# Recommender kernel: recorded instructions with semaphores of the kernel's own, and six more columns of token rows fetched by SyncE and ScalarE

## The chip, the cores and the metric

One core of a Trainium2 chip runs the program. A core has five engines that run side by side: TensorE (PE), VectorE (DVE), ScalarE (ACT), GpSimd (POOL) and SyncE (SP), each with an instruction stream of its own, and 16 DMA engines that move data between the memory of the chip and the core. Engines wait for each other by semaphores. The metric is the device time of one execution in microseconds; lower is better.

## The reference

16,384 examples, each with 32 token indices, three lists of 20 indices and four single indices. What is computed:

```python
tok = word_emb[token_idx].mean(axis=1)          # 32 rows of 300 floats out of 50000, per example
e1, e2, e3 = emb_mh1[mh1_idx].mean(axis=1), ...  # 20 rows of 64 out of 1000, 5000, 10000
o1, o2, o3, o4 = emb_oh1[oh1_idx], ...           # one row of 64 each
emb = concatenate([tok, e1, e2, e3, o1, o2, o3, o4], axis=1)        # 748 wide
wide = sums of the one-column tables wide_mh*, wide_oh* at the same indices
h = relu(emb @ W1 + b1); h = relu(h @ W2 + b2); h = relu(h @ W3 + b3)   # 1024, 512, 256
return sigmoid(h @ Wd + bd + wide)
```

All in float32. The token rows are the bulk of what is moved: 16,384 x 32 rows of 1200 bytes.

## The kernel before, in words

The examples are cut into 128 tiles of 128, one example per partition. A tile takes 11 steps of a main loop of 1435 steps in all (27 of them are the end). In a step several things are emitted for different tiles, so that the engines overlap:

- **Small tables** are not gathered. Per step DVE builds one-hot rows (`one_hots`, tile `hot`), ACT scales a part of them in place (by 256), PE multiplies them into counts (`counts`, tile `pc`), and ACT evicts these to `cnt`. A tile later PE multiplies the counts with the tables on chip (`small_sums`, tile `pg`), and DVE reduces the result into the features `g`.
- **Token rows** come by `tokens()`. A column is one of the 32 token positions of a tile: 128 indices, one row of 300 floats for each partition. POOL issues one indirect DMA (a gather) per column into half of a `tok_rows` buffer; there are six buffers of two columns, and DVE adds the two halves of a pair into `tok_sum` (in tile `own`, `add_up`) three pairs later in program order. 1.42 pairs per step are emitted.
- **Fetched columns** spare POOL a gather. For some tiles SP (`fetch`, column 31) or ACT (`ScalarRows`, column 30) loads the 128 indices as offsets into registers (a TENSOR_LOAD of 32 or 8 values) and issues 128 DMAs of one row each, into `fetched` or `fetched_scalar`. Ahead of it the column of indices is loaded and DVE turns it into byte offsets (`column_offsets`). SP is paced at 128 rows in 16.5 steps. ACT's rows are put in wherever the next transfer would take one of two places of a count modulo 8 (`sync_dma`, `hardware_dma`).
- **Layers** (`mlp`) run for one to three tiles at once on PE in float32, with ACT evicting.

The order of every engine but POOL is that of the emitting code. The semaphores are the framework's: hardware transfers take eight of them in turn (LANES; SP's rows come to use 0 to 5, ACT's 6 and 7), the gathers eight others, and a transfer waits for the one before it in its lane.

## Time and profile before

| | |
|---|---|
| median of three runs | 7429.4 us (7415.1 to 7435.34) |
| span of the profiled execution, first to last instruction | 5019.3 us |
| time of that execution beside its span | not given; median less span is 2410.1 us |
| gathers on POOL | 3987, 946 ns each |
| row DMAs of SP, of ACT | 10624, 3328 |
| granted TensorE clock, mean | 0.990 |

The span covers the program's own instructions. Busy time counts the engines' work, not the issuing of a transfer by a sequencer and not waiting; rows with SPq or ACTq are such issues. "Idle before" is the time in which an engine did nothing ahead of an instruction, put down to the event that stood last before its start.

### The profile page before, as it was taken

To read this page: it belongs to the slowest core of one execution; us is meant where nothing else is said; L and a number is where in the kernel's file an instruction comes from. 1 tells how busy PE (TensorE), PEld (TensorE's weight loads), DVE (VectorE), ACT (ScalarE), POOL (GpSimd) and SP (SyncE) were. 2 spreads that over 40 slices of the span, in tenths; PEclk is the share of its full clock that TensorE was granted. 3 is DMA by queue.
4 is the path that set the end of the run, shared out by engine and by line. 5 is a ranking of instruction groups with operands and counts; after the bars stand their busy time and mean duration, and the time that the engine had idled before them with its cause. 6 is when DMAs were issued, how large, how long until landed. Compare 5 with 4: busy or idle time off the path is not lost.

```text
span 5019.3 us, 124363 instructions
## 1 busy us (share of the span) xinstructions
PE 4806.3 (96%) x36356; PEld 3721.3 (74%) x36356; DVE 3748.7 (75%) x6830; ACT 2726.5 (54%) x3658; POOL 3774.2 (75%) x3994
## 2 busy tenths in 40 slices
PE   6799999999999999999999999999999999999999
PEld 4577777777777777777777777667767888888899
DVE  6777777777777777777777777777777777777774
ACT  5455555555555555555555555555555555555552
POOL 7777777777777777777777777777777777777775
PEclk8899999999999999999999999999999999999999
DMA  7444444444444444444444444444444444444443
GB/s 204 127 129 130 129 129 129 129 130 129 129 130 128 129 130 129 130 129 129 129 129 129 130 129 129 130 129 129 130 130 129 129 129 130 130 129 130 129 128 100
DMA packets 291735, 654.13 MB, mean 130 GB/s; under 512 B 147100, under 2 KB 161692, under 8 KB 291048
## 3 DMA queue, kind: packets, MB, share of 16 engines
q0 software_dynamic: 191376, 612.66, 45.1%
q1 hardware_dynamic: 89271, 29.49, 2.7%
q10 hardware_dynamic: 10400, 4.02, 0.4%
q8 instruction: 284, 4.65, 0.4%
q14 instruction: 404, 3.30, 0.2%
HBM read 645.65 MB, written 0.07 MB: 129 GB/s over the span
## 4 chain that ended last, share of the span: by engine, by line
PE 37%; DMA 26%; DVE 15%; issue 12%; POOL 9%; ACT 1%; SPq 1%; ACTq 0%; DVEq 0%; POOLq 0%
DMA tok_rows<-in_word_emb_dram,it 23%; PE ph L677 17%; PE pg L554 14%; POOL tok_rows L337 9%; DVE hot L501 5%; DVE own L319 4%; PE pc L519 4%; DVE own L314 3%; DMA fetched_scalar<-in_word_emb_dram 1%; DMA fetched<-in_word_emb_dram 1%; PE pc L595 1%; DVE g L544 1%; PE po L719 1%; SPq L161 1%; DVE x L599 0%
## 5 line engine op out<-in xcount | busy, mean ns | idle before, releaser
L337 POOL DMA_INDIRECT tok_rows<-in_word_emb_dram,it x3987 | 3773.3, 946 | 1219.3 <-issue 754.1
L508 ACT ACTIVATE hot<-hot 64x768 bf16<-64x768 bf16 (+1 forms) x1408 | 1155.4, 821 | 1820.6 <-DVE hot L501 1664.0
L554 PE MATMUL pg<-terms,cnt 128*128 128x195 bf16 x17664 | 1723.7, 249 | 35.6 <-DVE g L544 35.0
L554 PEld LDWEIGHTS <-cnt 128*128 128x128 fp8e3 x17664 | 1529.2, 98 | 83.1 <-issue 54.4
L677 PE MATMUL ph<-x,w_sb 128*128 128x384 f32 (+5 forms) x4932 | 1473.8, 437 | 16.2 <-ACT h L688 11.9
L501 DVE TENSOR_TENSOR hot<-own,sc 128x1656 bf16<-128x1656 bf16 (+1 forms) x1408 | 1393.7, 990 | 126.7 <-PE pc L519 37.7
L522 ACT ACTIVATE cnt<-pc 128x828 uint16<-128x828 f32 (+1 forms) x1408 | 1186.5, 843 | 181.5 <-PE pc L519 103.2
L319 DVE TENSOR_TENSOR own<-own,tok_rows 128x300 f32<-128x300 f32 x1792 | 857.1, 478 | 513.3 <-DMA tok_rows<-in_word_emb_dram,it 468.5
L677 PE MATMUL ph<-h,w_sb 128*128 128x384 f32 (+2 forms) x4160 | 1225.9, 435 | 14.2 <-ACT h L688 14.0
L314 DVE TENSOR_TENSOR own<-own,tok_rows 128x300 f32<-128x300 f32 x1827 | 873.8, 478 | 271.9 <-DMA tok_rows<-in_word_emb_dram,it 221.0
L677 PEld LDWEIGHTS ph<-x,w_sb 128*128 128x128 f32 (+1 forms) x4932 | 830.8, 191 | 305.7 <-ACT h L688 23.0
L519 PEld LDWEIGHTS <-hot 128*128 128x128 bf16 x8192 | 594.2, 98 | 523.8 <-issue 271.3
L677 PEld LDWEIGHTS ph<-h,w_sb 128*128 128x128 f32 x4160 | 700.6, 191 | 266.1 <-ACT h L688 27.3
L519 PE MATMUL pc<-hot 128*128 128x138 bf16 x8192 | 733.1, 225 | 111.8 <-ACT hot L508 51.7
L688 ACT ACTIVATE h<-ph,b_sb 128x384 f32<-128x384 f32 (+2 forms) x723 | 378.7, 524 | 210.5 <-PE ph L677 115.4
L544 DVE TENSOR_REDUCE g<-pg 128x130 f32<-128x390 f32 (+1 forms) x512 | 259.2, 506 | 140.0 <-PE pg L554 138.7
L599 DVE TENSOR_TENSOR x<-pc,scale 128x768 f32<-128x768 f32 x127 | 120.8, 951 | 58.8 <-PE pc L595 57.5
L595 PE MATMUL pc<-ident,g 128*128 128x128 f32 x762 | 107.3, 278 | 5.7 <-ACT cnt L522 5.4
L312 DVE TENSOR_TENSOR own<-tok_rows 128x300 f32<-128x300 f32 x128 | 61.5, 481 | 55.3 <-DMA tok_rows<-in_word_emb_dram,it 52.6
L595 PEld LDWEIGHTS pc<-ident,g 128*128 128x128 f32 x762 | 83.7, 143 | 9.8 <-ACT cnt L522 9.3
L488 DVE COPY sc<-pc 128x512 bf16<-128x512 bf16 x64 | 44.0, 688 | 40.5 <-PE pc L484 39.8
L719 PE MATMUL po<-h,wd_sb 128*1 128x384 f32 (+2 forms) x208 | 67.4, 442 | 4.4 <-ACT h L688 4.4
(59 smaller groups left out, 514.6 us busy)
## 6 DMA issues: line engine op xcount, KB each, us to landing
fetched<-in_word_emb_dram SPq DMA_DIRECT2D x10624, 1.2 KB
tok_rows<-in_word_emb_dram,it POOLq DMA_INDIRECT x3987
fetched_scalar<-in_word_emb_dram ACTq DMA_DIRECT2D x3328, 1.2 KB
ix<-in_idx_dram SPq DMA_DIRECT2D x64, 64.0 KB
w_sb<-in_W_dram SPq DMA_DIRECT2D x6, 512.0 KB
raw<-in_mh_dram SPq DMA_DIRECT2D x4, 682.5 KB
it<-in_idx_dram SPq DMA_DIRECT2D x64, 32.0 KB
w_sb<-in_W_dram SPq DMA_DIRECT2D x1, 2048.0 KB
```

Source lines behind the costliest of these rows:

```text
L314: nc.vector.tensor_add(tok_sum, tok_sum, a)
L319: nc.vector.tensor_add(to, tok_sum, b)
L337: gather = nc.gpsimd.indirect_dma_start(out=rows[-1], out_offset=None, in_=word, in_offset=bass.IndirectOffsetOnAxis(ap=it[:, j : j + 1], ...
L501: nc.vector.tensor_tensor(hot[:, 0 : 2 * rows, :].rearrange("p i (n d) -> p i n d", d=2), iota.rearrange("p (n d) -> p n d", d=2).unsqueez ...
L508: nc.scalar.activation(upper, upper, AF.Copy, scale=UPPER)
L519: nc.tensor.matmul(pc[:, k // n, at : at + n_h], hot[:, 2 * k, 0:P], hot[:, 2 * k + 1, :], start=True, stop=True)
L522: nc.scalar.activation(cnt[:, :, b : b + rows].rearrange("l h (g k) -> l h g k", g=2), pc[:, :, 0 : n * n_h].rearrange("l g (k h) -> l h g ...
L544: nc.vector.tensor_reduce(field_columns(features(t), pair), pg[:, 0:n, :].rearrange("p f (c d) -> p f d c", c=3), AX.X, ALU.add,)
L554: nc.tensor.matmul(pg[:, j, :], by_slice[:, h, :], terms[:, h, :], start=(h == h0), stop=(h == h1 - 1))
L595: nc.tensor.transpose(pt[:, j // n, j % n, :], g[:, c : c + P], ident)
L677: nc.tensor.matmul(to, weights[: src.shape[0], k, m * P : (m + 1) * P], src, start=(k == 0), stop=(k == len(srcs) - 1),)
L688: nc.scalar.activation(dst()[:, m, 0:n], ph[:, 0:n], AF.Relu, bias=bias[:, m : m + 1])
```

## The change

All instructions are now recorded first, each with the regions that it reads and writes (`Program.record`), and then emitted in one block (`Program.emit`) with semaphores that the kernel allots itself. Per engine there is one semaphore, raised only by instructions that somebody waits for; a wait that is already implied by an earlier one is left out. The gathers have one semaphore per `tok_rows` buffer, which both gathers of a pair raise; rows of a fetched column have one of eight semaphores per engine, raised by all 128 rows, and no row waits for another. The other hardware transfers still take eight lanes in turn. PE's bf16 and fp8 weight loads are no longer entries of their own but part of their matmul.

SP and ACT are given their columns by a table made ahead (`RowFetches`): column after column without a pause, each for the first free tile that still leaves the margin. SP fetches 84 columns at the same 16.5 steps each; ACT 31, three rows in every step, two ahead of the scaling of `hot` and one behind it. 3981 gathers are left on POOL. The order of PE's matmuls and ACT's activations is that of before, and DVE's too but for the small offset instructions.

```diff
-    def hardware_dma(queue, **operands):
-        dma = queue.dma_start(**operands)
-        if transfers and transfers[-1][0] is not queue:
-            tc.add_manual_dep(...)
-        transfers.append((queue, dma.ins.name))
     def sync_dma(**operands):
-        while len(transfers) % LANES in SCALAR_LANES and scalar_row and scalar_row[0]():
-            pass
-        hardware_dma(nc.sync, **operands)
+        return program.dma(core.sync, **operands)
...
-                tok_rows = tokp.tile([P, TOK_GROUP * TOK_D], F32, name="tok_rows")
+                tok_rows, batch = tokp.next(), []
...
-                    gather = nc.gpsimd.indirect_dma_start(...)
-                    tc.stamp_issue_order_token(gather.ins, "gathers")
+                    program.gather(f"gather{tokp.slot}", rows[-1], word, it[:, j : j + 1], batch, tok_rows)
...
+    def gather(self, lane, out, table, index, batch, buffer):
+        def emit():
+            return self.nc.gpsimd.indirect_dma_start(...)
+        return self.record(emit, "POOL", lane, [index], [out if batch else buffer], batch=batch)
...
+        def need(other):
+            other = other.batch[-1]
+            if other.batch is ins.batch:
+                return
+            if other.stream == ins.stream and stream == "PE":
+                return
+            best = needed.get(other.stream)
+            if best is None or best.tick < other.tick:
+                needed[other.stream] = other
...
+        known = self.known[sequencer]
+        waits = [o for s, o in needed.items() if known.get(s, 0) < o.tick]
...
+    def fetch(t, j, by_scalar, loads):
+        queue, ring = (core.scalar, fa) if by_scalar else (core.sync, fp)
+        tile_rows = ring.next()
+        lane = f"{'ACT' if by_scalar else 'SP'}rows{rings[by_scalar] % ROW_SEMAPHORES}"
+        column, batch = columns.pop((t, j)), []
+        for p0 in range(0, P, loads):
+            values = program.load(queue, column[:, p0 : p0 + loads], last_offset)
+            yield 0
+            for p in range(p0, p0 + loads):
+                program.row(queue, lane, rows[p : p + 1, :], lambda values=values: values.pop(0), word_bytes, batch)
...
-    fetches = [(summed_at(t) - FETCH_AHEAD[t % 3], t) for t in range(FETCH_FROM, tiles) if t % 3]
+    by_sync = RowFetches(N_TOK - 1, False, summed_at(FETCH_FROM) - FETCH_STEPS - FETCH_MARGIN, FETCH_STEPS, tiles, LOADS)
+    by_scalar = RowFetches(
+        N_TOK - 2, True, int(summed_at(SCALAR_FROM) - scalar_steps - SCALAR_MARGIN), scalar_steps, tiles - 2, SCALAR_LOADS
+    )
...
+            by_sync.prepare(step)
+            by_scalar.prepare(step)
+            scalar_rows(step, SCALAR_BEFORE)
             if i < STEPS - 1:
                 hot = one_hots(sc, s, i + 1)
...
+            scalar_rows(step, SCALAR_AFTER)
-            fetch_rows(step, 0.5)
+            sync_rows.to(step + 0.5)
```

The first gathers of the program in POOL's queue, before (DMASW0 to 7 are the gathers' lanes, DMAHW0 that of the index transfer; the ending _49 belongs to the framework's names):

```order
L337 DMA tok_rows<-in_word_emb_dram,it 128x300 [waits DMAHW0_49]
L337 DMA tok_rows<-in_word_emb_dram,it 128x300 x7
L337 DMA tok_rows<-in_word_emb_dram,it 128x300 [waits DMASW0_49]
L337 DMA tok_rows<-in_word_emb_dram,it 128x300 [waits DMASW1_49]
L337 DMA tok_rows<-in_word_emb_dram,it 128x300 [waits DMASW2_49]
L337 DMA tok_rows<-in_word_emb_dram,it 128x300 [waits DMASW3_49]
L337 DMA tok_rows<-in_word_emb_dram,it 128x300 [waits DMASW4_49,DVE_49]
L337 DMA tok_rows<-in_word_emb_dram,it 128x300 [waits DMASW5_49]
L337 DMA tok_rows<-in_word_emb_dram,it 128x300 [waits DMASW6_49,DVE_49]
```

and the same place now (tok_rows_61 to 66 are the six buffers):

```order
L244 DMA tok_rows_61<-in_word_emb_dram,it_67 128x300 [waits sem_lane0]
L244 DMA tok_rows_61<-in_word_emb_dram,it_67 128x300
L244 DMA tok_rows_62<-in_word_emb_dram,it_67 128x300 x2
L244 DMA tok_rows_63<-in_word_emb_dram,it_67 128x300 x2
L244 DMA tok_rows_64<-in_word_emb_dram,it_67 128x300 x2
L244 DMA tok_rows_65<-in_word_emb_dram,it_67 128x300 x2
L244 DMA tok_rows_66<-in_word_emb_dram,it_67 128x300 x2
L244 DMA tok_rows_61<-in_word_emb_dram,it_67 128x300 [waits sem_DVE]
L244 DMA tok_rows_61<-in_word_emb_dram,it_67 128x300
```

Before, seven gathers follow the first without a wait, and from the ninth on each waits for the one eight places back, every second one for DVE too; now the first of a pair waits for DVE, and the second for nothing.

DVE in the middle of the program, before, where the two adds of a pair are the lines 314 and 319:

```order
L501 TENSOR_TENSOR hot<-own,sc 128x1656 [waits DVE_49,PE_49,Activation_49]
L314 TENSOR_TENSOR own<-own,tok_rows 128x300 [waits DMASW5_49,DVE_49]
L319 TENSOR_TENSOR own<-own,tok_rows 128x300 [waits DMASW6_49,DVE_49]
L314 TENSOR_TENSOR own<-own,tok_rows 128x300 [waits DMASW7_49,DVE_49]
L319 TENSOR_TENSOR own<-own,tok_rows 128x300 [waits DMASW0_49,DVE_49]
```

and now (all engines' instructions carry the line of the recorder, L112):

```order
L112 TENSOR_TENSOR hot_77<-own,sc_74 128x1656
L112 TENSOR_TENSOR own<-own,tok_rows_61 128x300 [waits sem_gather0,sem_DVE]
L112 TENSOR_TENSOR own<-own,tok_rows_61 128x300 [waits sem_DVE]
L112 TENSOR_TENSOR hot_76<-own,sc_74 128x1656 [waits sem_PE]
L112 TENSOR_TENSOR own<-own,tok_rows_62 128x300 [waits sem_gather1,sem_DVE]
```

Each add waited for its own gather; now the first add of a pair waits for both gathers, the second for DVE alone.

ACT in the middle of the program, before (DMAHW6 and 7 are the lanes left to it):

```order
L508 ACTIVATE hot<-hot 64x6x128 [waits DVE_49]
L375 TENSOR_LOAD columns
L688 ACTIVATE h_51810<-ph,b_sb 128x384 [waits PE_49]
L522 ACTIVATE cnt<-pc 128x138x6 [waits PE_49]
L161 DMA fetched_scalar<-in_word_emb_dram 1x1200 [waits DMAHW6_49]
L161 DMA fetched_scalar<-in_word_emb_dram 1x1200 [waits DMAHW7_49]
L508 ACTIVATE hot<-hot 64x6x128 [waits DVE_49]
```

and now (`odd` is the buffer of the first layer's result):

```order
L112 ACTIVATE cnt_78<-pc_94 128x138x6 [waits sem_ACT,sem_PE]
L238 DMA fetched_scalar_82<-in_word_emb_dram 1x1200 x2
L112 ACTIVATE hot_76<-hot_76 64x6x128 [waits sem_DVE]
L259 TENSOR_LOAD columns
L238 DMA fetched_scalar_82<-in_word_emb_dram 1x1200
L112 ACTIVATE cnt_78<-pc_94 128x138x6 [waits sem_PE]
```

The rows have lost their waits and stand at fixed places around `hot`; most count evictions have got a wait for an earlier one of ACT's own.

533 lines of the change are left out of this document (353 added, 180 removed).

## Prediction

> **What bounds the kernel now.** I read the page's head first, then the groups of instructions, then the timeline of POOL, and only then the waits of the other engines. The page's head:
>
> ```profile
> span 5019.3 us, 124363 instructions
> PE 4806.3 (96%) x36356; PEld 3721.3 (74%) x36356; DVE 3748.7 (75%) x6830; ACT 2726.5 (54%) x3658; POOL 3774.2 (75%) x3994
> ```
>
> By busy time PE looks like the bound (4806.3 of 5019.3) and POOL like an engine with a quarter to spare. The groups and the view of one tile, `tok_rows`, say otherwise (columns of the first: count, busy us, mean ns, idle before it; of the second: shortest/median/longest ns, first and last start in us):
>
> ```profile
> L337 POOL DMA_INDIRECT tok_rows<-in_word_emb_dram,it x3987 | 3773.3, 946 | 1219.3 <-issue 754.1 <-DVE own L319 222.3 <-DVE own L314 78.3
> ...
> L337 POOL DMA_INDIRECT tok_rows<-in_word_emb_dram,it x3987: 942/946/1233, 2.8 to 4993.1; - x200
> ```
>
> Idle time of 1219.3 us over 3987 gathers is 0.306 us for each, and from the first start to the last there are (4993.1 - 2.8) / 3986 = 1.252 us per gather. So is the idle time a wait? The waits of POOL, and its timeline at the start of the program, answer it:
>
> ```profile
> POOL tok_rows L337 <- issue: 754.1, 2473, 0.3
> POOL tok_rows L337 <- DVE own L319: 222.3, 721, 2.7
> POOL tok_rows L337 <- DVE own L314: 78.3, 257, 0.3
> ...
> 2.84 1.10 POOL L337 DMA_INDIRECT tok_rows<-in_word_emb_dram,it  x1 [1.36 <-DMA it<-in_idx_dram]
> 4.25 0.95 POOL L337 DMA_INDIRECT tok_rows<-in_word_emb_dram,it  x1 [0.30 <-issue]
> 5.50 0.94 POOL L337 DMA_INDIRECT tok_rows<-in_word_emb_dram,it  x1 [0.30 <-issue]
> 6.74 0.94 POOL L337 DMA_INDIRECT tok_rows<-in_word_emb_dram,it  x1 [0.30 <-issue]
> ...
> 12.99 0.95 POOL L337 DMA_INDIRECT tok_rows<-in_word_emb_dram,it  x1 [0.30 <-issue]
> 14.24 0.94 POOL L337 DMA_INDIRECT tok_rows<-in_word_emb_dram,it  x1 [0.30 <-issue]
> ```
>
> Nearly every gap is 0.30 us whichever event stands beside it, and 721 gaps "for DVE" hold 222.3 us, 0.308 each. The first eight gathers, which wait for no buffer and no earlier gather (the order of POOL shows it), stand at the same 1.25 us as the later ones that wait for one or two semaphores. So 1.25 us is what a gather costs POOL, and POOL issues without a pause from 2.8 us to 4993.1 us: 3986 x 1.25 = 4982.5 of the 4990.3 us between. What is over, some 8 us, has one visible piece near the end:
>
> ```profile
> 4929.22 0.95 POOL L337 DMA_INDIRECT tok_rows<-in_word_emb_dram,it  x1 [0.30 <-issue]
> 4932.82 0.94 POOL L337 DMA_INDIRECT tok_rows<-in_word_emb_dram,it  x1 [2.65 <-DVE own L319]
> ```
>
> The span is then 2.8 us of start, 4990.3 us of gathers, and 26.2 us after the last gather's start, in which the last tile goes through the layers. Everything else follows POOL: DVE, which adds the rows up, sits waiting for rows to land, and ACT waits for DVE.
>
> ```profile
> DVE own L319 <- DMA tok_rows<-in_word_emb_dram,it: 468.5, 683, 2.8
> DVE own L314 <- DMA tok_rows<-in_word_emb_dram,it: 221.0, 333, 3.1
> ...
> ACT hot L508 <- DVE hot L501: 1664.0, 1089, 5.0
> ...
> 2000.00:2500.00 500.00, 488.05 (x3557) 358.57 (x3555) 378.71 (x688) 274.05 (x356) 378.02 (x401) 0.99 0.48 129
> ```
>
> The last row (a stretch of 500 us: PE, PEld, DVE, ACT, POOL busy, then PE clock, DMA share, GB/s) has 401 gathers in 500 us, 1.247 each, with PE at 488 of 500. PE is the next bound, 2.4% behind.
>
> **What lies around the span.** The page gives no time of the profiled execution besides its span. The median of the runs shown is 7429.4 us, 2410.1 us above that span, and no row of the trace shows what fills the difference. I carry it over as a constant; what it could do otherwise is a rival below. The page "Runtime: NRT & Kernel Launch" of the Trainium skill, section "The ~15µs preamble/postamble breakdown", puts about 9 to 15 us around a kernel, which as an estimate from that page would make the time some 5034 us; the runs measured 7429.4, so the measurement decides, and the page doesn't explain the rest.
>
> **The change, part by part.** *Fewer gathers.* SP fetches 84 columns instead of 83 (10624 rows in the trace / 128), ACT 31 instead of 26 (3328 / 128), so POOL issues 4096 - 115 = 3981 gathers instead of 3987. Six gathers at 1.25 us are 7.5 us, all of it on the bound. The place of a fetched column doesn't matter, as POOL has no other work to wait for.
>
> *Fewer semaphores on POOL.* Of 2032 wait-only instructions 1973 go, and the second gather of a pair waits for nothing. Bounds: nothing, by the eight gathers at the start that have no waits and the same 1.25 us; and, from the other side, all 0.306 us of every gap. The rows at 4.25 to 6.74 us are the very thing that the change makes of the others, so I take zero; the other end is a rival.
>
> *One semaphore for a pair.* Before, the first add of a pair waits for its own gather; now both adds wait for both. The second gather's landing and its add:
>
> ```profile
> 4969.32 2.90 DMA tok_rows<-in_word_emb_dram,it
> 4972.22 0.03 issue
> 4972.26 0.04 issue
> 4972.31 0.49 DVE own L319
> ```
>
> The pair was done 3.5 us after the second gather's start, 4.7 us after the first's. Now the first add (0.48 us) stands behind the landing too, so the pair is done 0.5 us later. Its buffer is wanted again six pairs later, 15 us after the first gather's start, so some 10 us of cover become 9.7. DVE's next work also shifts by 0.5 us, once, as a lag and not as a rate. Cost: zero while the cover holds; at the one place where it doesn't, the 2.65 us stall above, up to 0.5 us more.
>
> *ACT's queue.* Before, its rows went into two lanes that other transfers pass through too, and its activations stood behind rows that waited there; SP's rows waited for theirs:
>
> ```profile
> ACT hot L508 <- DMA fetched_scalar<-in_word_emb_dram: 95.1, 92, 3.0
> ACT h L688 <- DMA fetched_scalar<-in_word_emb_dram: 62.9, 84, 1.7
> ACT cnt L522 <- DMA fetched_scalar<-in_word_emb_dram: 49.8, 67, 1.6
> ...
> SPq L161 <- DMA fetched<-in_word_emb_dram: 132.3, 541, 0.6
> ```
>
> These 207.8 us of ACT and 132.3 of SP go. Against that, ACT issues 640 more rows, 80 more loads of offsets, and a wait of its own before most count evictions. Prices:
>
> ```profile
> L161 ACTq DMA_DIRECT2D fetched_scalar<-in_word_emb_dram x3328: 213/214/746, 309.9 to 4790.8; - x196
> L375 ACTq TENSOR_LOAD <-columns x416: 716/763/1013, 307.0 to 4770.6; - x139
> ...
> 2000.23 0.84 ACT L508 ACTIVATE hot<-hot 64x768 bf16<-64x768 bf16 x1 [2.19 <-DVE hot L501]
> 2000.31 0.77 ACTq L161 DMA_DIRECT2D fetched_scalar<-in_word_emb_dram  x2
> 2001.13 0.87 ACT L522 ACTIVATE cnt<-pc 128x828 uint16<-128x828 f32 x1
> ```
>
> Two rows take 0.77 us and lie wholly beside the 0.84 us of `hot`; the next activation starts on time. Three rows a step are at most 1.2 us, a load every 2.67 steps 0.29, the activations 2726.5 / 1435 = 1.9 us, together 3.4 of a step's 3.5 us (5019.3 / 1435) even with nothing overlapped. Neither the gain nor the cost reaches POOL, because ACT's 1664.0 us of waiting for DVE cover both. I take zero, with plus and minus 10 us as what a few late steps would leave.
>
> *SP.* It now has no lane to wait for, and the same pace:
>
> ```profile
> 2014.39 12.77 SPq L161 DMA_DIRECT2D fetched<-in_word_emb_dram  x31
> ```
>
> 0.41 us a row with its share of offset loads makes 53 us a column, against 16.5 steps x 3.5 = 57.7 us. It keeps up, as it did.
>
> *PE.* The bf16 and fp8 weight loads are no longer separate entries, so a wait now holds a weight load together with its matmul. 2424 matmuls have a wait; were each to lose a load that ran ahead (98 ns), it would be 238 us, more than the 213 us that PE is idle. But most of them are f32 matmuls and transposes that were joined before, and in a stream the loads run beside the matmul before. Of the 1408 count steps the first matmul alone is affected, and it stood behind `hot` anyway. I take zero.
>
> *Start and end.* One more hand-over at the start: the whole program is one block now, entered by a branch on each engine. Bounds 0.3 us (the gap behind the barrier in POOL's first rows) to 3 us (the whole of today's start is 2.8); I take 1 us. The end is the same chain, and the columns of the last tile are all gathered.
>
> **Sum.** 5019.3 - 7.5 + 1 = 5012.8 us of span; with 2410.1 us around it, 7422.9. I say 7423 us. One rule of the Trainium skill speaks against any gain: "DMA: Bandwidth & Descriptors", section "Issuing engines are not separate DMA queues", says that starting transfers from several engines saves only the sequencer's issue time, usually small beside the transfer. By it the six moved columns would bring nothing, 7429.4. Here the row differs: 1.25 us of issue per gather is the bound and the DMA share is 0.48.
>
> **Rivals.** *A gather gets cheaper* (the 0.306 us gaps were semaphores). Then PE would be the bound: 4806.3 busy plus a start and an end like today's (2.8 + 26.2) and some 30 us of its own waits, about 4870: 7280. For: 1973 wait-only instructions do go. Against: the first eight gathers. 6%.
>
> *What lies around the span shrinks with the program.* In the built programs the change takes out 5067 wait-only instructions and adds about 1650 for rows and loads: 3420 of 124363, 2.75%. If the 2410 us go with the length, that is 66 us: 7356. For: nothing in the trace fills these 2410 us. Against: nothing says that they follow the length. 12%.
>
> *ACT becomes the slow path (slower).* Rows and loads now stand at fixed places, two rows ahead of `hot` and one behind it, whatever ACT is late with; a load of 0.76 us lands ahead of `hot` or `cnt` in the queue, and the counts on PE wait for these. PE has 2.4% to give, 0.084 us a step or 120 us over 1435 steps. 496 loads x 0.76 = 377 us, so it decides once a third of them is exposed; at half of them the time is 68 us longer than forecast, 7490; at all of them 257 us, 7680. Against: the timeline, where loads and rows hide, and 207.8 us of lane waits that go. 14%.
>
> *It doesn't reach the time.* The columns go as said but the unprofiled runs are held by something that the profiled one isn't, so the six gathers count for nothing: 7429. It falls on the same side as the forecast and shares its chance.
>
> **Chances and range.** Runs of the kernel before lie 20 us apart, and 0.3% (22 us) is about what can be told from no change. Forecast with its last rival 60%, all of it within 0.3% but for 4% on each side; cheaper gathers 6%, a shorter surround 12%, slow ACT 14%; the remaining 8% I split between unexplained gains (4%) and losses (4%). Faster: 4 + 6 + 12 + 4 = 26%; slower: 4 + 14 + 4 = 22%; same: 52%. The forecast's own range is 7410 to 7436. To hold 8 in 10 it must take in the shorter surround and the near part of the slow ACT: 7350 to 7460.
>
> **What would show it.** POOL's gathers x3981 with a gap of 0.30 us and a span near 5013 show the first two steps right; a gap of 0.2 or less shows the first rival. Lines of ACT waiting for `fetched_scalar` should be gone, and DVE's waits for `tok_rows` should move from two lines to the first add of a pair. POOL idle for DVE by more than 10 us in all, or more `PEld` idle behind `hot`, would speak for the third rival. A span near 5013 with a time off by more than 22 us would put the cause around the span. Wrong altogether is the forecast if gathers stay at 1.25 us and the span still moves by over 20 us.

## The result, and the profile after

| kernel | median us | lowest, highest | runs |
|---|---|---|---|
| before | 7429.4 | 7415.1, 7435.3 | 3 |
| after | 7340.7 | 7320.1, 7342.5 | 3 |

The ratio is 0.9889 with a 95% interval of 0.9853 to 0.9925: faster by 1.1%, 88.7 us, where 7423 (7350 to 7460) was forecast. The head of the changed kernel's page, from a run of 7342.49 us, and below it the granted clock and the chain that ended last:

```profile
span 7340.7 us, 120941 instructions
PE 5626.2 (77%) x36356; PEld 4090.5 (56%) x36356; DVE 3616.7 (49%) x6842; ACT 2735.9 (37%) x3658; POOL 3769.9 (51%) x3988
...
PEclk7798888888889888888888888888888988888888
...
PE 50%; another core or an unknown queue 18%; issue 15%; DVE 14%; ACT 2%; ACTq 1%; DMA 0%; DVEq 0%; SPq 0%
```

The first thing to see is the span: 7340.7 of 7342.5 us. **Nothing lies around the span**; 1.8 us do. The 2410.1 us that the prediction set there are inside the execution, which is another kind of execution than the profiled one of before: the mean granted clock is 0.873, not 0.990, and each engine is idle for a larger share (POOL 51% busy, before 75%). The gathers among the page's groups (busy us and mean ns, then idle before them), and from the view of all waits those of POOL, ACT and DVE (us in total, times, longest us):

```profile
L244 POOL DMA_INDIRECT tok_rows<-in_word_emb_dram,it x3981 | 3769.0, 947 | 3517.6 <-DVE own L112 2278.9
```

```profile
POOL tok_rows L244 <- DVE own L112: 2278.9, 755, 19.6
ACT cnt L112 <- remote: 1563.5, 277, 11.4
...
DVE hot L112 <- remote: 1087.0, 190, 10.0
```

A gather still takes 947 ns and usually follows after 0.30 us, but 543 times POOL stands for over 2 us until DVE frees a buffer (the 755 of the row hold usual gaps too), and DVE and ACT wait for a release that the view can't name ("remote"). The chain that ended last has no POOL in it. What the release is, one place of the changed kernel's timeline shows (start us, us, engine, instruction, idle time before it and its releaser):

```profile
3000.88 0.25 PE L112 MATMUL pg<-terms,cnt 128*128 128x195 bf16 x1
...
3004.61 0.53 PE L112 MATMUL pc<-hot 128*128 128x138 bf16 x6
...
3007.67 0.94 POOL L244 DMA_INDIRECT tok_rows<-in_word_emb_dram,it  x1 [0.30 <-issue]
3010.66 0.36 DVE L112 TENSOR_REDUCE g<-pg 128x65 f32<-128x195 f32 x1 [9.32 <-remote]
...
3011.08 2.80 PE L112 MATMUL pg<-terms,cnt 128*128 128x195 bf16 x16 [5.95 <-issue]
3011.44 0.86 ACT L112 ACTIVATE cnt<-pc 128x828 uint16<-128x828 f32 x1 [10.13 <-remote]
...
3013.63 0.94 POOL L244 DMA_INDIRECT tok_rows<-in_word_emb_dram,it  x1 [5.02 <-DVE own L112]
```

The reduction at 3010.66 reads what the matmul at 3000.88 made, whose row ends at 3001.13. It gets the signal 9.5 us later: the semaphore records of TensorE show none between 2998.43 and 3010.64 us, though its rows go on to 3005.1. **TensorE gave no signal for 12 us.** How much of this it stood still the records don't tell: the rows up to 3005.1 carry four signals, spread over 4.0 us, and all four come within 1.0 us, from 3010.64 to 3011.61; no row starts between 3004.9 and 3011.08. DVE and ACT stop within 3 us, and when the six pair buffers are full, POOL stops too, for 5.02 us.

I call such a pause a halt. Counted over the trace (pauses of over 4 us between two signals in which a signalling matmul's row had ended 3 us before), there are 464 halts with a median of 8.3 us. Some signal records are missing, so the count is rough, and a pause holds some work too. What the halts cost shows in TensorE's rows, held against the full-clock run e2 below: they take 815 us more (5626.2 and 4811.3), gaps in which TensorE waits for nothing that the trace shows come to 937 us (none there), and its waits for DVE and ACT grow from 198 to 761 us, together 2315 of the 2320 us between the spans. For 294 of the halts a stretch of half clock begins inside the halt or within 4 us behind it, in the median 0.7 us before it ends; in all there are 298 such stretches, and 170 halts go without one. The half clock therefore follows the halt and isn't its cause. "TensorE: Matmul & The Clock Gate" of the Trainium skill, section "What's actually happening", says the same of the clock (idle for a window of some 3.4 us takes it to one half), and the trace agrees: 247 of the 298 stretches last 3.4 or 6.8 us. What holds TensorE up in the first place neither the trace nor that section tells.

### The profile page after: what moved, and what is told of

Read it like the earlier page. It is cut to its first block, busy times and chain, and to the rows that moved or that the text cites. A ratio compares the mean times of both kernels' runs of the same rounds, so it can differ in the third digit from the quotient of the medians.

```text
span 7340.7 us, 120941 instructions
## 1 busy us (share of the span) xinstructions
PE 5626.2 (77%) x36356; PEld 4090.5 (56%) x36356; DVE 3616.7 (49%) x6842; ACT 2735.9 (37%) x3658; POOL 3769.9 (51%) x3988
## 4 chain that ended last, share of the span: by engine, by line
PE 50%; another core or an unknown queue 18%; issue 15%; DVE 14%; ACT 2%; ACTq 1%; DMA 0%; DVEq 0%; SPq 0%
PE ph L112 22%; PE pg L112 21%; PE pc L112 7%; DVE own L112 6%; DVE hot L112 6%; DVE g L112 2%; ACT hot L112 1%; ACT cnt L112 1%; ACTq L238 1%; DVE columns L112 0%; ACT odd L112 0%; ACTq L259 0%; DVE x L112 0%; DVE keys L112 0%
## 5 line engine op out<-in xcount | busy, mean ns | idle before, releaser
L112 PE MATMUL pg<-terms,cnt 128*128 128x195 bf16 x17664 | 2102.8, 270 | 938.8 <-issue 630.1
L112 PEld LDWEIGHTS pg<-terms,cnt 128*128 128x128 fp8e3 x17664 | 1690.1, 106 | 1186.1 <-issue 797.5
L112 DVE TENSOR_TENSOR hot<-own,sc 128x1656 bf16<-128x1656 bf16 (+1 forms) x1408 | 1390.0, 987 | 1486.3 <-remote 1087.0
L112 ACT ACTIVATE cnt<-pc 128x828 uint16<-128x828 f32 (+1 forms) x1408 | 1185.6, 842 | 2175.0 <-remote 1563.5
L112 DVE TENSOR_TENSOR own<-own,tok_rows 128x300 f32<-128x300 f32 x3619 | 1719.0, 475 | 95.3 <-DMA tok_rows<-in_word_emb_dram,it 14.3
L112 PE MATMUL ph<-x,w_sb 128*128 128x384 f32 (+5 forms) x4932 | 1652.1, 474 | 138.0 <-issue 82.0
L112 ACT ACTIVATE hot<-hot 64x768 bf16<-64x768 bf16 (+1 forms) x1408 | 1155.2, 820 | 1616.0 <-DVE hot L112 1343.1
L112 PEld LDWEIGHTS ph<-x,w_sb 128*128 128x128 f32 (+1 forms) x4932 | 918.4, 211 | 501.6 <-issue 191.3
L112 PE MATMUL ph<-odd,w_sb 128*128 128x384 f32 (+2 forms) x3328 | 1084.1, 465 | 76.4 <-issue 52.7
L112 PEld LDWEIGHTS pc<-hot 128*128 128x128 bf16 x8192 | 634.4, 104 | 868.8 <-issue 404.5
L112 PE MATMUL pc<-hot 128*128 128x138 bf16 x8192 | 807.0, 236 | 373.0 <-ACT hot L112 214.9
L112 DVE TENSOR_REDUCE g<-pg 128x130 f32<-128x390 f32 (+1 forms) x512 | 261.0, 510 | 1476.7 <-remote 881.8
L112 PEld LDWEIGHTS ph<-odd,w_sb 128*128 128x128 f32 x3328 | 607.0, 207 | 320.4 <-issue 119.4
L112 ACT ACTIVATE odd<-ph,b_sb 128x384 f32<-128x384 f32 (+2 forms) x515 | 269.7, 524 | 422.7 <-remote 260.6
L112 PE MATMUL ph<-even,w_sb 128*128 128x384 f32 (+2 forms) x832 | 272.7, 463 | 63.5 <-ACT even L112 49.3
L112 DVE TENSOR_TENSOR x<-pc,scale 128x768 f32<-128x768 f32 x127 | 121.2, 954 | 333.1 <-PE pc L112 207.7
L112 PEld LDWEIGHTS ph<-even,w_sb 128*128 128x128 f32 x832 | 151.2, 203 | 129.8 <-ACT even L112 55.2
L112 ACT ACTIVATE even<-ph,b_sb 128x384 f32<-128x384 f32 (+2 forms) x208 | 108.5, 523 | 212.5 <-remote 130.2
L112 DVE COPY sc<-pc 128x512 bf16<-128x512 bf16 x64 | 44.2, 691 | 254.8 <-PE pc L112 178.3
L112 PE MATMUL pc<-ident,g 128*128 128x128 f32 x762 | 124.5, 306 | 40.2 <-ACT cnt L112 23.8
L112 PEld LDWEIGHTS pc<-ident,g 128*128 128x128 f32 x762 | 98.4, 161 | 46.6 <-ACT cnt L112 25.6
```

What stands on the lines that cost most here:

```text
L112: lambda: call(*args, **operands), self.name, self.name, aps + list(named.values()), outs
```

## The experiments

"Clock" is the mean granted clock of the run; each ratio is to the kernel before, run beside it on the same chip.

| run | what | clock | us | before, beside it | ratio (95%) |
|---|---|---|---|---|---|
| e1 | before | 0.990 | 5022.8 | 5022.7 | 0.9999 (0.9990 to 1.0009) |
| e2 | after | 0.989 | 5023.0 | 5022.7 | 1.0000 (0.9990 to 1.0010) |
| e3 | after, 83 and 26 columns | 0.990 | 5031.1 | 5022.7 | 1.0015 (1.0006 to 1.0025) |
| e4 | after, half contraction | 0.985 | 5246.6 | 5022.7 | 1.0444 (1.0419 to 1.0470) |
| e13 | after | 0.989 | 5021.0 | 5021.0 | 1.0000 (0.9990 to 1.0010) |
| e11 | after, waits on POOL | 0.989 | 5022.1 | 5021.0 | 1.0002 (0.9992 to 1.0012) |
| e12 | after, twice the waits on DVE | 0.990 | 5024.6 | 5021.0 | 1.0008 (0.9998 to 1.0017) |
| e14 | after, early drain | 0.991 | 5014.1 | 5021.0 | 0.9987 (0.9977 to 0.9996) |
| e5 | after, early drain | 0.878 | 7235.7 | 7335.8 | 0.9859 (0.9829 to 0.9890) |
| e6 | before, bursts on PE | 0.955 | 8167.6 | 7335.8 | 1.1139 (1.1110 to 1.1167) |
| e7 | after, bursts on PE | 0.959 | 8093.3 | 7335.8 | 1.1021 (1.0996 to 1.1046) |
| e8 | before | 0.873 | 7422.8 | 7423.0 | 0.9997 (0.9982 to 1.0012) |
| e9 | after, 83 and 26 columns | 0.879 | 7304.3 | 7423.0 | 0.9828 (0.9787 to 0.9869) |
| e10 | after, waits on DVE | 0.870 | 7431.3 | 7423.0 | 1.0009 (0.9984 to 1.0035) |
| e15 | after, waits on POOL | 0.868 | 7372.5 | 7329.2 | 1.0058 (1.0041 to 1.0075) |
| e16 | after, twice the waits on DVE | 0.875 | 7368.7 | 7329.2 | 1.0054 (1.0036 to 1.0072) |
| e17 | after | 0.875 | 7345.5 | 7418.4 | 0.9906 (0.9872 to 0.9939) |
| e18 | after, waits on POOL | 0.866 | 7471.0 | 7418.4 | 1.0069 (1.0044 to 1.0093) |

The two groups are two kinds of chip: on two chips the kernel before has medians of 5021.0 and 5022.7 us, on three others of 7329 to 7423. The profile shown of before is like the first kind, its times are like the second. I call them full-clock and halting chips. Whether it belongs to the chip or to its state at the time isn't shown; the one chip that came twice (e8 to e10, e17 and e18) halted both times.

### Before and after at full clock

No edit.

> The kernel before, unchanged, for a profile in the regime of the timed runs (the profile shown of it ran 5019.3 us, the timed runs 7429.4). Theory A, the TensorE clock: the changed kernel's trace has 298 stretches of half clock (1872 us in all), and in the microseconds ahead of each PE, DVE and ACT all but stop; so here a time of 7429 +- 20 us, a mean granted clock of 0.86 to 0.88 in place of 0.990, some 300 to 310 such stretches, and POOL idle for DVE, which the page of 5019.3 us does not have. Theory B, the length of the program: 7429 us too, but with about as many half-clock stretches as in the changed kernel and idle time that goes with the instruction count. Theory C, work around the span: a span near 5019 us with a time of 7429.

> The changed kernel again, beside the next two. All theories: 7341 +- 25 us, ratio to before 0.985 to 0.993, granted clock 0.87.

Both came to a full-clock chip: 5022.8 and 5023.0, no difference. The head of the changed kernel's page there, to be held against the one of 7340.7 us:

```profile
span 5021.1 us, 120941 instructions
PE 4811.3 (96%) x36356; PEld 3713.7 (74%) x36356; DVE 3628.4 (72%) x6842; ACT 2729.1 (54%) x3658; POOL 3771.3 (75%) x3988
...
PEclk9899999999999999999999999999999999999999
...
PE 31%; DMA 24%; POOL 19%; DVE 15%; issue 9%; ACT 1%; ACTq 0%; DVEq 0%; SPq 0%; POOLq 0%
```

The same program, the same POOL work of 3771 us, PE at 96% and a span 2320 us shorter. POOL and the landing of its rows hold 43% of the chain that ended last. The theories on the low clock could not be tried there, but the prediction's sum could, term by term. Of before, the gathers in the view of their tile (count, shortest/median/longest ns, first and last start in us) and then, from the timeline, the last store:

```profile
L337 POOL DMA_INDIRECT tok_rows<-in_word_emb_dram,it x3987: 940/946/1242, 3.0 to 4995.5; - x200
```

```profile
5019.51 0.22 SPq L161 DMA_DIRECT2D out_dram<-x  x1
```

The last store of after, also from its timeline:

```profile
5012.31 0.22 SPq L232 DMA_DIRECT2D out_dram<-x  x1
```

The gathers of after go from 3.2 to 4989.2 us. So they end 6.3 us sooner: 7.5 for six gathers, less 1 us of stalls and 0.2 of a later start. The last store comes 7.2 us sooner (5019.51 and 5012.31). Yet the spans are 5021.6 and 5021.1: 2.1 us stand behind the last store before, 8.8 after. The rows there are no busy time and stand in the raw records (start in us, ns):

```
before  4988.82  12965  POOL DRAIN
after   5013.74   6272  POOL DRAIN
```

POOL drains its queue for 6.27 us, and in the recorded program this stands in the hand-over behind the last store, where all wait for it; before, POOL drained beside the last tile's layers.

### The recorder without the columns

```diff
             self.due.append((start, t))
             start = end
+        drop = (3, 9, 15, 21, 27) if by_scalar else (len(self.due) - 1,)
+        self.due = [d for k, d in enumerate(self.due) if k not in drop]
```

> The changed kernel with the columns of before: SyncE fetches 83 in place of 84, ScalarE 26 in place of 31, so POOL issues 3987 gathers again; the recorded instructions stay. Theory A: POOL is not the bound at a lower clock, so the same as the changed kernel, 7341 +- 20 us, ratio 0.985 to 0.993. The theory of the prediction (1.25 us a gather on the bound): 7349. If the gain comes from moved columns alone: 7429. Theory B (time goes with the instruction count, 768 rows and 84 offset loads fewer, some 850 to 1600 instructions less of 120941): 7240 to 7290.

At full clock 5031.1, 8.0 us above the changed kernel beside it: six gathers at 1.25 us are 7.5. The step of the prediction that priced the columns was right at full clock, and the rest of the change costs 8.4 us there, most of it the drain at the end (below).

> The changed kernel with the 83 and 26 columns of before, again, for a chip that takes the clock down. Where it does not, the recorded instructions alone cost 8.4 us (5031.1 against 5022.7) and the six columns bring them back. Where it does: if POOL is no bound there, the columns bring nothing and this takes what the changed kernel takes, ratio to before 0.984 to 0.993; if the columns are the gain, 1.000 +- 0.004.

On a halting chip it has a ratio of 0.9828 (7304.3 us); the changed kernel has 0.9906 on the same chip later (e17, 7345.5 us) and 0.9889 in the result. The six columns bring nothing there and may cost something: the intervals of e9 and e17 just don't overlap (to 0.9869, from 0.9872). All of the gain comes from the rest of the change: the recorder with its semaphores, the new places of the fetched rows, and a part not told so far, that TensorE's result buffers `pc` and `ph` are now handed out by which is free (`Banks`). These three were not run apart.

### Half of the contraction

```diff
-                weights[: src.shape[0], k, m * P : (m + 1) * P], src,
+                weights[:half, k, m * P : (m + 1) * P], src[:half],    # half = src.shape[0] // 2
```

> The changed kernel with every matmul of the three layers contracting over half of its rows (64 partitions in place of 128): the second half of each inner product is left out, while the number of instructions, their columns and their waits stay. Theory A, if the clock follows what TensorE switches: fewer half-clock stretches, a mean clock over 0.93 and a time well below 7000 us, at best 5013. Theory A, if the clock follows only how long TensorE is busy: 7341 +- 25 us with 0.87. Theory B: 7341 +- 25 us.

A miss. It came to a full-clock chip, where there are no halts to take away, and it was slower: PE 5141.2 us busy in place of 4811.3, 98% of the span. Its largest group of layer matmuls and that of e2, by form (busy us, mean ns):

```profile
L112 PE MATMUL ph<-x,w_sb 64*128 64x384 f32 x2560 | 991.0, 510 | 0.0
```

```profile
L112 PE MATMUL ph<-x,w_sb 128*128 128x384 f32 x2560 | 944.5, 493 | 2.9 <-ACT odd L112 2.4 <-DVE x L112 0.5
```

510 ns over 64 rows, 493 over 128. Halved rows are not cheaper, and why the whole got dearer I did not follow up. Whether less switching would avoid the halts stays untested.

### The drain at the end

```diff
+            self.nc.gpsimd.drain()          # behind POOL's last gather
             wait(self.engines["SP"], last)
```

> The changed kernel with one instruction more: POOL drains right behind its last gather, while the last tile goes through the layers, and not for the first time in the hand-over at the very end, where the changed kernel's trace has a DRAIN of 6272 ns behind the last store (13.74 us ahead of it the kernel before has its DRAIN, of 12950 ns, at 4986 us, beside other work). If that drain is what the recorded program pays at its end: 6 us less than the changed kernel at a clock near 0.99, 5017 +- 1.5 us where the kernel before takes 5023 (ratio 0.9988). If a drain costs 6.3 us whenever it comes: the changed kernel's time, 5023. On a chip that grants a clock of 0.87 the same 6 us in some 7341, too little to be seen.

> The changed kernel, unchanged, beside the next three. Where the chip takes the clock down: ratio to before 0.985 to 0.993 (measured so far: 0.9889, without the six columns 0.9828). Where it does not: 1.000 +- 0.001.

> The changed kernel with POOL's drain right behind its last gather, again: at a clock of 0.99 5016.5 +- 1.5 us (ratio 0.9988), as the DRAIN of 6272 ns leaves the end of the program; where the clock is taken down, 6 us below the changed kernel run beside it, inside the noise of 20 us.

At full clock 5014.1 beside 5021.0 for the changed kernel: 6.8 us, near the 6 expected; the time itself lies 0.9 us under the expected 5015 to 5018, since this chip takes 5021.0 and not 5023 for the kernel before. The early drain takes 17137 ns beside the layers and the one in the hand-over then 41 ns. On a halting chip the ratio is 0.9859, not to be told from the changed kernel's. This version is ahead of the kernel before on both kinds of chip, by 0.1% and by 1.4%.

### Bursts on TensorE

```diff
+                repeats = HALTS if k == 0 and m % 2 else 1            # 13
+                for again in range(repeats):
                     nc.tensor.matmul(..., stop=(k == len(srcs) - 1 or again < repeats - 1))
```

> The kernel before, with TensorE made late in bursts: in every second output of a layer the first matmul is done 13 times, so that some 364 times PE is 1.7 to 6 us late (4368 matmuls more, by the trace's 493, 386 and 278 ns some 1900 us more of PE). Where the result stands is not changed. It stands for a chip whose TensorE halts some 300 times for several us, as in the changed kernel's trace at 7340.7 us. Theory A: both programs then follow PE and time is lost around each burst as well; if the old program's waits make it recover worse, this one takes 1 to 2% longer than the next run. Otherwise (the difference of 1.2% is not one of waiting for PE): both within 0.3% of one another. Estimate of the time itself: PE 4806 + 1900 + idle, 6750 to 6900 us.

> The changed kernel with the same bursts. Theory A (the recorded program recovers faster from a late PE): 1 to 2% below the run before. Otherwise: the same within 0.3%, some 6750 to 6900 us.

The recorded program is 74 us (0.9%) ahead here too, just below the 1 to 2% of theory A. But both came to a halting chip, so the bursts did not stand alone, and the absolute times missed (8168 and 8093 against 6750 to 6900). The bursts are as large as planned: PE 7433.3 us busy in place of the 5632.2 of e8. Yet the time of before grew by only 832 us beside the plain kernel, with 110 stretches of half clock (114 in e7) where e8 has 319. Denser work on TensorE didn't bring more of them, but fewer. The two runs say that the gain doesn't hang on one pattern of late TensorE, no more.

### Waits put back on VectorE

```diff
+                if ins.sequencer == "DVE":
+                    old = waits[:1] or old
+                    seen += 1
+                    if old and not waits and seen % 2:
+                        wait(engine, old)
+                    elif waits:
+                        wait(engine, waits[:1])
                 wait(engine, waits[len(on_it) :])
```

> The kernel before, unchanged, for its trace on a chip that takes TensorE's clock down (a first look was on a chip that did not: 5022.8 us at 0.990; the kernel before then took 7336 on another, beside 7429 in the runs of the prediction). On such a chip: 7336 +- 40 us, a mean granted clock of 0.870 to 0.875, 290 to 310 stretches of half clock, and PE idle with 'issue' as its reason. Theory A1 (the recorded program loses less in each stretch): as many stretches as the changed kernel (298 in the trace of 7340.7 us, 285 with the early drain), but more time in each. Theory A2 (the changed kernel gets fewer stretches): in proportion, 3 to 5 more than 1% above the changed kernel's count. On a chip that does not: 5023 +- 3 us.

> The changed kernel with waits put back on VectorE: nearly every second of its instructions waits once more, for what it has already waited for, some 3500 wait-only instructions, about as many as the change took out (5487 to 1889). The result and the order stay. If the gain at a low clock comes from VectorE's waits (theory A1 with DVE as the place): the gain is gone, ratio to before 0.995 to 1.005. If these waits cost nothing, since DVE waits for PE anyway: the changed kernel's ratio, 0.984 to 0.993. Where the clock is not taken down: 5023 to 5026 us.

The before of e8 and the changed kernel of e17 ran on the same chip. The head of e8's page:

```profile
span 7418.4 us, 124363 instructions
PE 5632.2 (76%) x36356; PEld 4118.0 (56%) x36356; DVE 3771.5 (51%) x6830; ACT 2740.8 (37%) x3658; POOL 3776.6 (51%) x3994
...
PEclk8788888888888888888888888888888888888888
```

The kernel before is thus held up in the same way: each engine's busy time is nearly that of the changed kernel but for DVE's (3771.5 and 3616.7 in the run of 7342.49). The gathers in the view of their tile, of before and then of after:

```profile
L337 POOL DMA_INDIRECT tok_rows<-in_word_emb_dram,it x3987: 940/947/1203, 3.0 to 7369.4; - x200
```

```profile
L244 POOL DMA_INDIRECT tok_rows<-in_word_emb_dram,it x3981: 940/947/1234, 3.2 to 7277.8; - x200
```

POOL's waits for DVE are split over several lines before (the adds of L312, L314, L319) and stand on one after, so these can't be set side by side; first and last start can. Before: 7366.4 us, of which 3986 x 1.25 = 4982.5, and 2383.9 beyond the pace. After: 7274.6, 4975.0 and 2299.6. So POOL's account of the 87.4 us between the spans (7418.4 and 7331.0) is 7.5 for the six gathers, 84.3 for shorter stalls, and -4.4 for the start and the end. **This is not yet a cause**, since in these runs POOL waits for DVE and next to nothing waits for POOL. DVE's waits for token rows, in e17 and then at full clock, in e2:

```profile
DVE own L112 <- DMA tok_rows<-in_word_emb_dram,it: 12.3, 9, 1.7
```

```profile
DVE own L112 <- DMA tok_rows<-in_word_emb_dram,it: 994.7, 1013, 4.1
```

At full clock DVE waits 994.7 us for rows, on the halting chip 12.3. There the rows lie ready, the chain that ended last has no POOL in it, and six gathers more made e9 no slower: what sets the time is TensorE with its halts, and DVE and ACT that wait for it and that it waits for. TensorE's own account (us, from the views of its waits):

| trace | rows | idle, no wait shown | waits for DVE and ACT |
|---|---|---|---|
| before (e8) | 5632 | 934 | 842 |
| after (e17; the run of 7342.49) | 5631; 5626 | 979; 937 | 705; 761 |
| e9, without the columns | 5619 | 988 | 690 |
| e10, waits on DVE | 5673 | 967 | 759 |
| e18, waits on POOL | 5676 | 1047 | 736 |
| full clock, before (e1), after (e2) | 4806, 4811 | 0, 0 | 211, 198 |
| bursts, before (e6), after (e7) | 7433, 7414 | 486, 507 | 236, 164 |

The changed kernel's gain shows in the last column: TensorE waits 137 and 81 us less for DVE and ACT. The two runs of that kernel lie up to 56 us apart in a column, so smaller differences can't be read. Within it, the waits of `pc` for DVE fall from 152 us (e8) to 9 (e17), while those for ACT rise from 194 to 279. DVE itself has become quicker between its instructions. Its timeline where it starts again, of before and of after:

```profile
3022.39 1.02 DVE L501 TENSOR_TENSOR hot<-own,sc 128x1656 bf16<-128x1656 bf16 x1 [7.67 <-remote]
3023.45 0.48 DVE L314 TENSOR_TENSOR own<-own,tok_rows 128x300 f32<-128x300 f32 x1
3023.96 0.48 DVE L319 TENSOR_TENSOR own<-own,tok_rows 128x300 f32<-128x300 f32 x1
```

```profile
3023.96 1.02 DVE L112 TENSOR_TENSOR hot<-own,sc 128x1656 bf16<-128x1656 bf16 x1 [4.65 <-remote]
3024.89 2.01 DVE L112 TENSOR_TENSOR own<-own,tok_rows 128x300 f32<-128x300 f32 x4
```

Before, the first add starts 1.06 us after the comparison's start (1053 ns in the median of e8), after the change 0.93 (928 in e17): the add now begins 83 ns before the comparison's row ends, and began 34 ns behind it. The wait-only instruction between them is not the reason. The kernel before takes 1044 ns where none stands there (514 places) and 1055 where one does (611); the changed kernel takes 927 without (896 places) and 937 with one (321). From an add to the next comparison it is 612 and 387 ns (medians at full clock, e1 and e2). Which part of the change makes VectorE start sooner the runs don't separate. I also measured, in each stall of POOL of over 2 us, the time from DVE's first instruction after it stood to the gather that starts again.

| trace | stalls over 2 us | mean stall, us | DVE's restart to gather, mean us |
|---|---|---|---|
| before (e8) | 544 | 4.43 | 2.82 |
| after (e17; the run of 7342.49) | 536; 543 | 4.37; 4.34 | 2.68; 2.67 |
| e9, without the columns | 535 | 4.33 | 2.66 |
| e10, waits on DVE | 535 | 4.48 | 2.76 |
| e16, twice the waits | 522 | 4.49 | 2.85 |
| e18, waits on POOL | 517 | 4.78 | 3.22 |

0.14 us x 540 stalls = 76 us, near the 84 above, but the two numbers don't prove each other: the stalls themselves are only 0.06 to 0.09 us shorter in the mean, and by the same sum e18 would lose 0.54 us x 517 = 279 us, where it loses 125 (below).

And e10, in which only waits on DVE are put back (6212 wait-only instructions in place of 1889), has no gain left: 1.0009, beside 0.9906 for the changed kernel on the same chip. POOL's time beyond the pace is 2382.6 us, as before, by the view of its tile:

```profile
L244 POOL DMA_INDIRECT tok_rows<-in_word_emb_dram,it x3981: 940/946/1242, 3.1 to 7360.7; - x200
```

One pair of adds in the timeline of e10, and one in that of e17:

```profile
3008.57 1.05 DVE L112 TENSOR_TENSOR own<-own,tok_rows 128x300 f32<-128x300 f32 x2
```

```profile
3012.25 0.98 DVE L112 TENSOR_TENSOR own<-own,tok_rows 128x300 f32<-128x300 f32 x2
```

With the wait of the second add standing in an instruction of its own as well, two adds are 0.07 us further apart (572 ns from start to start in the median, 504 in e17). "VectorE: DVE Perf Modes" of the Trainium skill, section "The DRAIN you can't avoid", says that a semaphore between chained operations costs nothing extra, by eight copies. Here both kernels have one between the adds, and what costs is the wait-only instruction, which that measurement doesn't have.

From a comparison to an add, though, e10 takes 928 ns, as the changed kernel does and not as the 1053 of before, and from an add to an add the kernel before takes 513. So e10 slows VectorE in another place than the kernel before. It shows that delays on VectorE alone can take the whole gain away; that VectorE's waits are what the change gained by is likely but not shown. So theory A1 has its place supported and its mechanism open. A2's count goes along (319 stretches of half clock before, 298 and 299 after, 315 in e10), which is cause or consequence, and these runs don't tell which; the number of halts doesn't (459 in e8 and 469 in e17, by the count above).

### Twice the waits, and waits on POOL

```diff
+                    if waits or old and seen % 2:
+                        wait(engine, old)
+                        wait(engine, old)
```

> Twice the dose on VectorE: two extra waits where the earlier kernel had one, some 8650 wait-only instructions in place of 4323. With one each the ratio to before was 1.0009 against 0.9889 for the changed kernel, 1.2%; theory 'place' and theory 'number' both give another 0.8 to 1.5%, a ratio of 1.008 to 1.017; if only the presence of a wait counts (whether VectorE may begin an instruction before the one ahead has ended), and not its time: 1.001 +- 0.004. Where the clock is not taken down: 5023 to 5040 us, as VectorE waits there for rows.

> Two extra waits on VectorE where the earlier kernel had one, again, for a chip that takes the clock down (where it does not: 1.0008 against 1.000 for the changed kernel). Time per wait: ratio to before 1.008 to 1.020. Only the presence of a wait: 1.001 +- 0.004.

At full clock 3.6 us above the changed kernel beside it, since DVE waits for rows there. On a halting chip 1.0054: between the two expectations (1.008 and more, 1.001 with 0.004 to either side), above the single dose's 1.0009 on another chip, with intervals that just don't overlap (to 1.0035, from 1.0036). The loss grows with the number of waits, if the changed kernel stands near 0.990 on that chip as on the others, where it wasn't run. The second dose is also no full dose: the traces of e12 and e16 have 8416 wait-only instructions on DVE, 2204 more than e10, where the first dose was 4323. That it adds less than the first says nothing by itself.

```diff
+                if ins.sequencer == "POOL":
+                    old = waits[:1] or old
+                    if old:
+                        wait(engine, old)
                 wait(engine, waits[len(on_it) :])
```

> The changed kernel with one more wait ahead of every gather, on POOL, for what POOL has already waited for: some 3980 wait-only instructions, nearly as many as the last kernel put on VectorE (4323). Theory 'place' (the gain at a low clock is VectorE's time: behind a hot comparison the next add starts 1055 ns after it before, 927 ns after the change, and a hot comparison behind an add 612 and 387 ns): POOL has 2300 us of idle time there, so the changed kernel's ratio, 0.984 to 0.993. Theory 'number' (each instruction costs, wherever it is): 0.996 to 1.004. Where the clock is not taken down, it tests the prediction's second step, that a satisfied wait costs POOL nothing in its 0.306 us gap: 5023 +- 2 us if so; with 20 to 70 ns each in full, 5100 to 5300 us.

> The waits on POOL again, for a chip that takes the clock down (where it does not, they cost 1.1 us beside the changed kernel). Theory 'place': ratio to before 0.980 to 0.993, as the changed kernel's and the one without the six columns'. Theory 'number': 0.996 to 1.004.

> The changed kernel beside the next run, on one chip: where the clock is taken down, ratio to before 0.980 to 0.993; where not, 1.000 +- 0.001.

> The waits on POOL again, with the changed kernel beside them. They had a ratio to before of 1.0058, on a chip on which the changed kernel itself was not run. Theory 'number': 1.2 to 2% above the changed kernel in this call. Theory 'place' (VectorE alone): within 0.4% of it; then the 1.0058 was that chip's. Where the clock is not taken down: within 0.1%.

At full clock the waits (2005 wait-only instructions on POOL in place of 59; gathers that had no wait carry one now) cost 1.1 us: a wait that is satisfied costs a gather nothing. That is the prediction's second step, shown. On halting chips they cost as much as the whole change brings and more: 1.0058 in e15, outside both expectations, and in e18 1.0069 beside 0.9906 on the same chip, 125 us or 1.7%. So VectorE isn't the only place, and theory "place" as I had put it falls. Theory "number" has its 1.2 to 2%, but falls as well by the price: 1946 instructions cost 125 us here, 65 ns each, and 4323 on DVE some 80 us, 19 ns each. The trace of e18 shows what changes at POOL. Its gathers take as long as ever, and the last starts 143.6 us later than that of e17 (7277.8):

```profile
L244 POOL DMA_INDIRECT tok_rows<-in_word_emb_dram,it x3981: 940/946/1239, 3.9 to 7421.4; - x200
```

In the changed kernel the gather that ends a stall starts some 270 ns after the end of the add that freed its buffer, in 95% of the stalls over 2 us (98% before). With the wait split off into an instruction ahead of the gather, it starts some 777 ns after it in 97% of them; summed over the stalls, that is 256 us more than in e17. The loss of 125 us is half of that, and DVE waits for rows no longer than in e17 (12.6 and 12.3 us). So the later gathers alone don't explain it: by TensorE's account its rows are 45 us longer, its idle time without a shown wait 68 and its waits for DVE and ACT 31, and how a wait on POOL comes to that stays open. (Before, a wait-only instruction stands ahead of the gather too, but the wait for DVE is on the gather; between the two there are 208 ns before and 724 in e18. What POOL does in these 724 no row shows.)

So much holds for the halting chips: **POOL's pace, the bound at full clock, isn't the bound there; TensorE with its halts, and DVE and ACT in a loop with it, are, and short delays on DVE or POOL cost 1 to 2%.** Which of the delays that the change removed makes its 1.1%, and what holds TensorE up, isn't shown. A deeper ring than six pairs wasn't tried.

## Why the prediction was wrong

- **The step that failed** is "What lies around the span": 2410.1 us "carried over as a constant". There is no such piece (1.8 us). The profile of 5019.3 us and the times of 7429.4 are two kinds of execution, and 2410 us between them was a sign that the rows at hand did not describe the timed runs. Granted clock and idle shares of the timed runs were unknown, and the forecast's own range of +-13 us claimed to know them.
- With it fell the **bound**. "1.25 us of issue per gather is the bound" is right for the profile of 5019.3 us (e2: DVE waits 994.7 us for rows) and wrong for the timed runs (12.3 us in e17). The six gathers, the only gain in the sum, brought nothing there (e9 without them: 7304.3 us, the changed kernel on the same chip 7345.5), and the 88.7 us came from what the sum had at zero. That the measured time lies on the forecast's side of 7429.4 is therefore luck.
- **A term left out**: VectorE. The part on semaphores dealt with POOL's, whose 1973 go without effect, with ACT's, SP's and PE's; DVE's waits, which fall from 5487 to 1889 and are the most of all, were counted only in the program's length. At full clock their price is zero, as DVE waits for rows; on a halting chip waits put back on DVE take the whole gain (e10, 1.0009). TensorE's waits for DVE and ACT fall there by 137 us (81 in the run of 7342.49), but which part of the change does that isn't separated.
- *Six gathers, 7.5 us*: right at full clock (8.0 between e2 and e3), nothing on a halting chip (e9).
- *POOL's semaphores, zero*: right at full clock (e11, 1.1 us).
- *One semaphore per pair, zero*: fits; the stalls at full clock grew by 1 us in all.
- *ACT and SP, zero*: fits at full clock. ACT's waits for `fetched_scalar` are gone from its list of waits.
- *Start +1 us*: +0.2. *The end is the same chain*: wrong by 6.3 us, POOL's drain. So at full clock the span changed by -0.5 us (5021.6 to 5021.1) where the sum had -6.5, and its "no change" came out through an error as large as the gain it had right.
- *Rival "cheaper gather"*: wrong, the gap is 0.30 us as before. *Rival "the surround shrinks with the program"*: 7356, nearest to 7340.7, but there is no surround and it isn't the program's length (65 and 19 ns per instruction by where it stands). *Rival "ACT"*: small; TensorE's waits for ACT rise from 111 to 146 us at full clock, and nothing reaches the time. *"It doesn't reach the time"*: right about the six gathers, as the timed runs were held by something else, but the rest of the change reached that.
- The test that the prediction set, "wrong altogether if gathers stay at 1.25 us and the span still moves by over 20 us", is what came out on halting chips.

## What to carry to other kernels

Before a profile is used to price a change, its span has to be near the time that is to be forecast; if it isn't, the missing time is the first thing to explain, and a range must hold both executions. An engine that waits in the profile may be in the loop that sets the time in another execution, so a wait that is free at full clock may cost there. An engine's stalls can add up to the difference of two runs and still be its consequence: before they are called the cause, look at who waits for that engine. Wrapping a program in one block can put a drain at its very end; drain the slow queue as soon as its last transfer is issued.

## What the runs showed of the hardware that I had not expected

- On three of the five chips that the runs came to TensorE gave no signal for several microseconds some 460 times in 7340 us (8.3 us in the median, some work included), in a program that has next to none of it on the others (4 by the same count). Its rows run on for some microseconds into such a halt, so the engines that wait for it stop first in the profile, with "remote" as their reason, and the half clock comes last. What sets off a halt stays open.
- A drain of POOL takes 6.27 us behind the last store and 41 ns where an earlier one has been done.
- In the changed kernel VectorE begins the add behind a comparison 83 ns before that row ends, with or without a wait-only instruction between them (937 and 927 ns from start to start); in the kernel before 34 ns behind it, again with or without one (1055 and 1044).
- A gather that waits for DVE itself starts 270 ns behind its release; with that wait in an instruction of its own ahead of it, 777 ns in 97% of the stalls.
